# Order of two products in the middle of a Strassen pair: A12's product with B21 moved ahead of the second sum's product

## The chip, the cores and the metric

The kernel runs on one NeuronCore of a Trainium2 chip. The metric is device time in microseconds (us) for one launch; the figure for the kernel before is the median of three runs. The engines are named as the profile names them: PE (TensorE matmuls), PEld (its weight loads), DVE (VectorE), ACT (ScalarE), POOL (GpSimd) and SP (SyncE, whose queue issues nearly all DMAs).

## The reference, cut to what matters

```python
scale = cond @ norm_w.T + 1.0
ms = mean(x * x, axis=-1)
h = x * (scale[:, None, :] * rsqrt(ms + EPS))     # x: (4, 1024, 512)
val, gate = split(h @ up_w.T, 2, axis=-1)         # up_w: (4096, 512)
h = val * gelu(gate)                              # (4, 1024, 2048)
hq = act_quant(h)                                 # per token: round(h * 127 / max|h|), scaled back
wq = weight_quant(down_w)                         # -1, 0 or 1 times one scale
y = hq @ wq.T                                     # down_w: (512, 2048)
return y + x
```

## The kernel before, in words

The four batch items are handled one after the other. For each, the 2048 hidden features are cut in 16 blocks of 128; one block of one item is a slot (`slot`, line 648), and all 1024 tokens of the item go through it as two halves of 512. Item 0 runs with plain matmuls (`plain_half`); items 1 to 3 run the up-projection as a Strassen-Winograd scheme of 7 products per slot instead of 8. Each such product (`product`, line 574; matmuls at line 580) is six matmuls of 128x512 into a PSUM bank called A, B or E.

The down-projection of an item is done while a later item's slots run. It is a Strassen-Winograd scheme too (class `Pair`, line 812). One pair takes 128 tokens of each half (A11, A12 are the first half's quantized features 0 to 1023 and 1024 to 2047; A21, A22 the second half's) and the ternary weight blocks B11, B12, B21, B22, with sums of activations S1 to S4 (`sum1` at line 827, `sums` at lines 834 to 836, all on DVE) and sums of weights T1 to T4. Each of its seven products (`Pair.product`, line 839; matmuls at line 848) is eight matmuls of 128x256, one half of a PSUM bank. A pair has three banks k1, k2, k3 of one pool of three ("po" in the profile), and goes in four steps:

- `first`: S1·T1 into k3's first half, A11·B11 into k3's second half; ACT copies the latter into both halves of k1 (line 858).
- `third`: S2·T2 is added to k1's second half; ACT copies that half into k2's second half (line 865); A12·B21 is added to k1's first half; DVE adds k3's first half to the two residual tiles xr (line 889, twice).
- `fourth`: S4·B22 into k1's second half, S3·T3 into k2's second half; ACT copies that into k2's first half (line 875); DVE adds k1 to xr (line 889).
- `fifth`: A22·T4 into k2's first half; DVE adds k2 to xr (line 889); SP stores both tiles (line 884).

Each engine works through its own queue in the order of the program text; a wait holds whatever stands behind it on that engine. A writer of a PSUM tile waits for earlier readers of that tile, also where the halves differ.

There are eleven pairs. Items 0 and 1 have four each, in slots 10 to 13 of items 1 and 2. In such a slot PE runs: `first`, up-products 0, 4 and 1, product 3 of the slot before, product 5, `third`, product 2 of the slot before (into E), `fourth`, product 6, `fifth`. ACT runs, around `third`, the copy of A at line 658 (after product 5), the copy of line 865, and then work of the next item's tokens that a planner (`Filler`, line 1204) hands out: squares (line 514), scaling (line 526), and high parts (line 559). POOL multiplies what line 526 leaves (line 527) and forms sums (lines 535 to 538). DVE has, besides the pair's steps, the maxima of the quantization (lines 714, 716) and the low parts of the next tokens (line 563) between its own steps of the slot (lines 678, 688, 694, 697). `next_pair` (line 1353) puts S1 of the next pair on DVE right after `fourth`.

Item 2 has three pairs, "old", after the last slot (lines 1432 to 1502). Between `third` and `fourth` of old pair 0 stands `first` of old pair 1; of old pair 1, `fifth` of pair 0, product 2 and `first` of pair 2; of old pair 2, `fifth` of pair 1 and eight plain matmuls of line 800. The fourth tile of item 2 and all of item 3 use plain matmuls (line 800). The kernel ends with item 3's quantization (lines 772 to 784) beside these matmuls ("po_end").

Of the kernel before, what the change touches and what calls it, by code (L numbers as in the profile page):

```python
# [50 lines left out]
def glu_quant_kernel(  # L51
# [760 lines left out]
    class Pair:  # L812
# [47 lines left out]
        def third(self, xrs, dq):  # L860

            k1, k2, k3 = self.banks
            self.xrs, self.dq = xrs, dq
            self.product(self.s[2], "T2", k1, 1, False, True)
            ACT.copy(k2[:, HALF:], k1[:, HALF:])  # L865
            self.product(self.part(0, 1), "B21", k1, 0, False, True)
            for h in range(2):
                self.onto(h, k3[:, :HALF], slice(HALF, D))

# [697 lines left out]
```

## Time and profile before

| what | value |
|---|---|
| median of 3 runs | 736.64 us (736.18 to 737.06) |
| the profiled execution's own time | 738.6 us |
| its span, first to last instruction | 736.8 us |
| mean granted TensorE clock | 0.997 |
| DVE busy | 580.1 us (79%), 819 instructions |
| ACT busy | 399.5 us (54%), 629 instructions |
| POOL busy | 195.8 us (27%), 207 instructions |
| line 848, matmuls of 128x256 | 269 to 283 ns each, median 272 or 273 |
| line 865, ACT copies of 128x256 | 11, 357 to 358 ns each, from 286.2 to 693.9 us |
| line 858, ACT copies of 128x512 in the first four pairs | 572 ns each |

How to read it: the span is the stretch that the trace covers; the medians come from runs without a profile, and a saving on the chain that ends last comes off either. A matmul's duration is longer than the distance at which the next one starts, because matmuls are pipelined; what a row of eight costs is read from the start of one row to the start of the next. A line of the timeline gives start, duration, engine, source line, operation, output and inputs, the count of merged instructions, and in brackets the idle time of that engine before it and what ended it.

### The profile page before, as it was taken

What the parts mean: (1) busy time and instruction counts of PE and PEld (TensorE: products, weight loads), DVE (VectorE), ACT (ScalarE), POOL (GpSimd) and SP (SyncE); (2) the same over time, 40 slices, a digit from 0 to 9 for tenths busy, and PEclk for the clock granted to TensorE, in tenths of its full rate; (3) what the DMA queues carried; (4) which work ended last, traced back from release to release, by engine and by line L of the source; (5) the groups of instructions that cost most, each with busy time, mean ns of one, the idle gap of its engine ahead of it and who ended that gap; (6) DMA issues with size and microseconds to landing.
All of it is one profiled execution on the core that took longest, in us unless ns stands there. A gap on an engine that the chain in (4) does not pass through costs nothing.

```text
span 736.8 us, 10143 instructions
## 1 busy us (share of the span) xinstructions
PE 721.8 (98%) x3662; PEld 360.4 (49%) x3662; DVE 580.1 (79%) x819; ACT 399.5 (54%) x629; POOL 195.8 (27%) x207
## 2 busy tenths in 40 slices
PE   6999999999999999999999999999999999999998
PEld 3544444444444446555444445665444444445744
DVE  5877888885698899787689897677678888756797
ACT  4868875872336674544335677443433666332264
POOL 1379887775100034340010031460020000000100
PEclk9999999999999999999999999999999999999999
DMA  6749999988344564766735647765934555442253
GB/s 225 257 130 324 279 276 264 246 204 228 115 101 101 129 147 132 196 169 152 184 100 102 130 102 180 190 148 147 231 94 105 88 118 101 101 100 86 99 175 114
DMA packets 203982, 117.30 MB, mean 159 GB/s; under 512 B 165382, under 2 KB 174487, under 8 KB 203932
## 3 DMA queue, kind: packets, MB, share of 16 engines
q1 hardware_dynamic: 203642, 116.33, 62.8%
q8 instruction: 28, 0.46, 0.3%
q10 hardware_dynamic: 290, 0.33, 0.1%
q14 instruction: 22, 0.18, 0.1%
HBM read 54.22 MB, written 23.09 MB: 105 GB/s over the span
## 4 chain that ended last, share of the span: by engine, by line
PE 89%; DVE 7%; DMA 1%; ACT 1%; issue 1%; SPq 0%; ACTq 0%; DVEq 0%
PE A L580 31%; PE E L580 16%; PE pg L595 10%; PE pv L595 10%; PE B L580 8%; PE po L848 8%; PE po_end L800 4%; DVE gm L714 1%; DVE R L716 1%; PE po L800 1%; DMA H<-in_x_dram 1%; PE ptx L939 1%; DVE R L709 1%; DMA SXY<-H 1%; DVE H L678 0%
## 5 line engine op out<-in xcount | busy, mean ns | idle before, releaser
L580 PEld LDWEIGHTS <-SXY 128*128 128x128 f16 x2016 | 197.2, 98 | 232.3 <-issue 0.7
L580 PE MATMUL A<-R,SXY 128*128 128x512 f16 x1152 | 266.3, 379 | 0.0
L580 PE MATMUL E<-R,SXY 128*128 128x512 f16 x576 | 140.0, 379 | 0.1
L678 DVE SCALAR_TENSOR_TENSOR H<-A,sg,t 128x512 f32<-128x512 f32 x48 | 36.0, 750 | 72.7 <-PE A L580 72.5
L730 POOL PARTITION_ALL_REDUCE am<-R x8 | 14.4, 1794 | 234.7 <-DVE R L716 234.7
L772 DVE TENSOR_TENSOR H<-H,am 128x1024 f32<-128x1024 f32 x64 | 76.2, 1217 | 0.0
L595 PEld LDWEIGHTS <-SXY 128*128 128x128 f16 x486 | 47.5, 98 | 57.5 <-DMA SXY<-H 0.8
L580 PE MATMUL B<-R,SXY 128*128 128x512 f16 x288 | 70.0, 379 | 0.0
L714 DVE TENSOR_REDUCE gm<-H 128x512 f32<-128x1024 f32 x56 | 69.0, 1233 | 1.0
L691 ACT ACTIVATE t<-t,sg 128x512 f32<-128x512 f32 x48 | 34.7, 724 | 63.9 <-DVE t L688 63.8
L595 PE MATMUL pg<-R,SXY 128*128 128x512 f16 x252 | 57.8, 379 | 0.3 <-DMA SXY<-H 0.3
L595 PE MATMUL pv<-R,SXY 128*128 128x512 f16 x234 | 54.4, 379 | 0.0
L848 PE MATMUL po<-wd,R 128*128 128x256 fp8e4 x384 | 49.7, 272 | 4.6 <-ACT po L865 4.6
L675 ACT ACTIVATE t<-B,sg 128x512 f32<-128x512 f32 x48 | 33.1, 689 | 36.4 <-PE B L580 36.4
L484 POOL TENSOR_SCALAR ssq<-ssq 128x2 f32<-128x2 f32 x12 | 4.2, 351 | 177.7 <-ACT xt L514 124.9
L658 ACT COPY t<-A 128x512 f32<-128x512 f32 x48 | 28.0, 584 | 39.4 <-PE A L580 39.1
L780 ACT ACTIVATE H<-H 128x1024 f32<-128x1024 f32 x38 | 40.0, 1052 | 15.6 <-DVE H L772 15.5
L848 PEld LDWEIGHTS <-R 128*128 128x128 bf16 (+1 forms) x416 | 40.6, 98 | 15.3 <-issue 7.0
L670 ACT COPY v<-E 128x512 f32<-128x512 f32 x48 | 28.2, 587 | 31.1 <-PE E L580 27.6
L716 DVE TENSOR_TENSOR R<-R,gm 128x512 f32<-128x512 f32 x56 | 42.7, 762 | 1.3
L697 DVE SCALAR_TENSOR_TENSOR H<-v,sg,t 128x512 f32<-128x512 f32 x48 | 37.5, 781 | 8.0 <-ACT t L691 8.0
L666 ACT COPY B<-A 128x512 f32<-128x512 f32 x48 | 27.5, 574 | 25.4 <-PE A L580 25.0
(208 smaller groups left out, 988.2 us busy)
## 6 DMA issues: line engine op xcount, KB each, us to landing
SXY<-s_dram SPq DMA_DIRECT2D x57, 256.0 KB, 3.1
s_dram<-SXY SPq DMA_DIRECT2D x18, 384.0 KB, 3.2
H<-in_L_cond_up_w_dram SPq DMA_DIRECT2D x13, 512.0 KB, 5.4
SXY<-s_dram SPq DMA_DIRECT2D x39, 128.0 KB, 3.1
xr<-in_x_dram SPq DMA_DIRECT2D x19, 256.0 KB, 3.0
out_dram<-xr SPq DMA_DIRECT2D x19, 256.0 KB, 2.4
H<-in_x_dram SPq DMA_DIRECT2D x8, 512.0 KB, 8.0
R<-in_L_cond_down_w_dram SPq DMA_DIRECT2D x8, 512.0 KB, 6.3
```

Source lines behind the costliest of these rows:

```text
L580: PE.matmul(o, s[:, w, k, :], tv[:, :, c, l, k, :], start=start and n == 0, stop=stop and n == len(TERMS) - 1, skip_group_check=True,)
L595: PE.matmul(ps, a[k // 2][:, w, k % 2, :], XP[:, l, k, h * TOK : (h + 1) * TOK], start=n == 0, stop=n == len(terms) - 1,)
L675: ACT.activation(cur["t1"], pb, AF.Gelu, scale=gain(g, 1))
L678: DVE.scalar_tensor_tensor(h_half(g - 1, 0), prev["A"], gain(g - 1, 0), prev["t1"], ALU.mult, ALU.mult)
L691: ACT.activation(prev["t2"], prev["t2"], AF.Gelu, scale=gain(g - 1, 1))
L697: DVE.scalar_tensor_tensor(h_half(g - 1, 1), prev["v"], gain(g - 1, 0), prev["t2"], ALU.mult, ALU.mult)
L714: DVE.tensor_reduce(gm[0], v, AX.X, ALU.max, apply_absolute_value=True)
L716: return [largest, lambda: DVE.tensor_tensor(m, m, gm[0], ALU.max)]
L772: DVE.tensor_tensor(v, v, r.to_broadcast([P, 2, TOK]), ALU.mult)
L780: ACT.activation(v, v, AF.Copy, bias=MAGIC)
L800: PE.matmul(po.rearrange("p (y c o) -> p y c o", c=2, o=P), q[:, a, h, j], wd8[:, :, j // n, j % n, :, y0:y1].rearrange("p c o y -> p y c o"),
L848: PE.matmul(po, w[:, j], m, start=start and j == 0, stop=stop and j == n - 1, skip_group_check=True,)
```

## The change

Inside `Pair.third` one line moves up. The product A12·B21 into k1's first half is issued first, then S2·T2 into k1's second half, and then the copy of that half into k2. The number and kind of instructions on every engine stay the same, and so does the order on DVE, POOL, SP and ACT. On PE two groups of eight matmuls, with their weight loads, change places in each of the eleven pairs. The copy's line number becomes 866.

```diff
             k1, k2, k3 = self.banks
             self.xrs, self.dq = xrs, dq
+            self.product(self.part(0, 1), "B21", k1, 0, False, True)
             self.product(self.s[2], "T2", k1, 1, False, True)
             ACT.copy(k2[:, HALF:], k1[:, HALF:])
-            self.product(self.part(0, 1), "B21", k1, 0, False, True)
             for h in range(2):
                 self.onto(h, k3[:, :HALF], slice(HALF, D))
```

In the list of instructions of the changed program, the semaphore wait for ACT that stood on the first matmul of A12·B21 stands on the first matmul of S4·B22 (in `fourth`) for the pairs inside slots.

## The prediction

> **What bounds the kernel.** I read the engines' shares, then the chain of work that ended last, then PE's waits, then the timeline around them.
>
> ```profile
> PE 721.8 (98%) x3662; PEld 360.4 (49%) x3662; DVE 580.1 (79%) x819; ACT 399.5 (54%) x629; POOL 195.8 (27%) x207
> ...
> PE 89%; DVE 7%; DMA 1%; ACT 1%; issue 1%; SPq 0%; ACTq 0%; DVEq 0%
> ```
>
> PE is busy for 98% of the span and carries 89% of the chain. So PE's few idle stretches are what can be won. The list of PE's waits (total us, times, longest):
>
> ```profile
> PE po L848 <- ACT po L865: 4.6, 10, 0.5
> PE ptx L939 <- DVE H L934: 2.8, 1, 2.8
> ...
> PE po_B L848 <- ACT po_A L865: 0.5, 1, 0.5
> ...
> PE po L848 <- DVE H L827: 0.3, 1, 0.3
> ```
>
> The largest one is the pair's own: eleven times, once per pair, PE waits for the copy of line 865. The timeline of the first pair's middle (slot 10 of item 1) shows who waits:
>
> ```profile
> 285.15 1.04 PE L848 MATMUL po<-wd,R 128*128 128x256 fp8e4 x8
> ...
> 286.23 0.36 ACT L865 COPY po<-po 128x256 f32<-128x256 f32 x1 [0.29 <-PE po L848]
> 286.50 1.34 ACT L526 ACTIVATE H<-H,rs 128x512 f32<-128x512 f32 x2
> 286.63 1.03 PE L848 MATMUL po<-wd,R 128*128 128x256 fp8e4 x8 [0.44 <-ACT po L865]
> ...
> 287.50 1.46 PE L580 MATMUL E<-R,SXY 128*128 128x512 f16 x6
> ...
> 288.80 1.04 PE L848 MATMUL po<-wd,H 128*128 128x256 fp8e4 x8
> ...
> 289.67 1.04 PE L848 MATMUL po<-wd,R 128*128 128x256 fp8e4 x8
> ...
> 290.80 0.36 ACT L875 COPY po<-po 128x256 f32<-128x256 f32 x1 [2.96 <-PE po L848]
> ```
>
> S2·T2 starts at 285.15; the copy waits for its end; A12·B21 writes the other half of the same bank and waits for the copy. Product 2 (E) and S4·B22 (288.80) follow without a gap.
>
> **What is removed.** Eight matmuls of line 848 cost 0.87 us from start to start (288.80 to 289.67). From S2·T2 to A12·B21 it is 286.63 - 285.15 = 1.48 us, so each middle loses 0.61 us. (The view's 0.44 leaves out 0.17 by which the last matmul normally overlaps its successor: 1.04 - 0.87.) The other seven pairs inside slots show 1.48 or 1.49; the three old pairs 1.53 or 1.54 (678.83 to 680.36, for one), a loss of 0.66. Together 8 x 0.61 + 3 x 0.66 = 6.86 us. With A12·B21 first no reader of k1 stands between the two products, and the stall goes.
>
> **What is added.** The next writer of k1 is S4·B22, which now waits for the copy. Counted from the start of `third`: before, the copy ended at 286.23 + 0.36 - 285.15 = 1.44. After, S2·T2 starts at 0.87, the copy ends at 2.31, product 2 starts at 1.74, takes 1.30 (287.50 to 288.80), and S4·B22 is due at 3.04. The cover is product 2 alone, with 0.73 us to spare; without it each pair would wait 0.57. In the old pairs at least sixteen matmuls (1.74 us) stand between, and the spare time is about 1.1. Cost: 0.
>
> **What moves on ACT.** The copy comes 0.87 us later after the start of `third`, and holds back what is queued behind it: line 526 or 559, then the copy of line 875, then the gelu of line 691. `fourth` comes 0.61 earlier, so ACT's idle time before line 875 shrinks by 1.48. It is 2.96, 1.19, 2.97 and 4.22 in item 1's four pairs and the same within 0.01 in item 2's. Only the pair in slot 11 falls short, by 0.29; A22·T4, which waits for that copy, starts 0.68 after it ended (307.62 against 306.58 + 0.36), so 0.39 is left. Cost: 0.
>
> **What moves elsewhere.** No DMA changes its place on SP. The DVE queue has the same order; line 889 after `third` reads k3, finished long before. S2 is wanted 0.87 later than before. POOL's line 527 follows ACT's line 526: 0.87 later in slot 10, 0.87 - 0.61 = 0.26 later in slot 11, 0.35 earlier in slot 12.
>
> **What is late next.** PE becomes earlier by 0.61 per pair; the question is whether DVE follows. In slots 11 and 12 of item 1 it hardly can:
>
> ```profile
> 305.69 0.48 DVE L889 SCALAR_TENSOR_TENSOR xr<-po,dq,xr 128x256 f32<-128x256 f32 x1 [0.41 <-DMA xr<-in_x_dram]
> ...
> 319.71 1.76 DVE L716 TENSOR_TENSOR R<-R,gm 128x512 f32<-128x512 f32 x1
> ...
> 323.44 1.21 DVE L827 TENSOR_TENSOR H<-R 128x1024 bf16<-128x1024 bf16 x1
> ...
> 324.70 1.05 PE L848 MATMUL po<-wd,H 128*128 128x256 fp8e4 x8 [0.26 <-DVE H L827]
> ...
> 488.18 0.75 DVE L678 SCALAR_TENSOR_TENSOR H<-A,sg,t 128x512 f32<-128x512 f32 x1 [1.91 <-PE A L580]
> ```
>
> From 305.69 to 324.65 DVE works with hardly a gap (0.13 us at 308.62), and S1 of the fourth pair (line 827) comes last: PE already waits for it before S1·T1 at 324.70. PE's own work would bring it there 3 x 0.61 + 0.42 = 2.25 earlier (0.42: 323.41 to 324.70 less 0.87). DVE's run begins with the landing of xr at 305.69. SP issues that load in an unbroken row of DMAs that begins at 292.04, when product 6 of slot 10 has ended, so it comes only slot 10's 0.61 earlier; with the gap of 0.13 closed DVE gains at most 0.74. But its operations there are stretched beside POOL (line 716 takes 1.76 where 0.69 is its usual time, line 827 takes 1.21 against 0.68), and POOL and DVE now shift by different amounts: one more meeting with a POOL sum (0.73 us each) would leave nothing. So S1·T1 of that pair comes between 0 and 0.74 earlier, with the far end at 0.7 later if two such meetings are added. I take 0.4, the middle of the two nearer ends, because both engines shift by parts of one slot only. With slot 13's own 0.61, item 1 gives 1.0 (bounds -0.1 and 1.35).
>
> The Trainium skill ("SBUF — State Buffer", "Who interferes with whom") says that a DVE instruction with two SBUF inputs and a GpSimd instruction that reads SBUF lock each other out for a whole instruction. The 1.76 of line 716 agrees: it ends 0.55 after POOL's operation does. Played through by that rule, POOL being 0.26 later in slot 11, lines 827 and 697 meet it anew and S1·T1 moves by about 0.3 (an estimate), which makes the sum 5.3 in place of 5.4.
>
> In item 2 DVE waits for PE in slot 12 (1.91 us before line 678, last row above), so it goes with PE again. The tight place is S1·T1 in slot 12, due at 481.92 - 1.22 = 480.70; line 827 ended at 480.49 and moves with xr, 0.61, unless POOL holds it, up to one operation of line 527 (1.25). I take nothing lost, 8 x 0.61 / 2 = 2.4; bound 1.9.
>
> The old pairs give 3 x 0.66 = 2.0. There DVE's steps follow PE: its idle time before line 889 is ended by PE at 688.27 (0.59), 698.93 (0.45) and 704.14 (0.33). After that DVE and ACT quantize with little idle time and PE's po_end matmuls never wait; should the quantization gain only what the first two pairs give it (1.24 at 688.27), 1.5 would be left, as PE needs its results within a few tenths of their making.
>
> Sum: 1.0 + 2.4 + 2.0 = 5.4 us. The profiled execution has 738.6 (span 736.8); its span would become 731.4. The median lies 0.2 under the span; 736.64 - 5.4 = **731.2 us**.
>
> **Rivals.** (1) Nothing becomes late: all 6.86 us come back, 729.8. For it: PE's waits on DVE sum to 0.3 in all slots. Against: the unbroken DVE run to 324.65.
> (2) More is late: DVE behind POOL's lock takes item 1's gain (0.6 left), one pair of item 2 loses its 0.61 and the end keeps 1.5: 0.6 + 1.8 + 1.5 = 3.9, 732.7. For it: the stretched rows. Against: DVE's idle time in item 2 and before each line 678 in slot 13 (3.13).
> (3) Slower: S4·B22 waits for the copy, since only product 2 covers it. It starts to wait once the copy is 0.73 late, and eats the gain from 1.34 on. At 2.0 late each pair in a slot loses 0.66: 8 x 0.66 less the old pairs' 2.0 is +3.3, 739.9. Against it: ACT was idle for 0.29 before this copy in all eight and waited for PE, and will stand idle longer now.
> (4) The change does nothing: PE's wait would have to move to S2·T2. Its first matmul has no new wait for ACT in the changed program; S4·B22 has it.
>
> **How the numbers follow.** Forecast 0.55; rival 1 0.22; rival 2 0.16; no change 0.04 (rival 4, or rival 3 in part); slower 0.03. Two kernels within 0.2% (1.5 us; the three runs differ by 0.9) can't be told apart. The first three lie beyond that: faster 0.93, same 0.04, slower 0.03. The range runs from rival 1 less half the runs' scatter, 729.4, to the low bounds together (-0.1 + 1.9 + 1.5 = 3.3, 733.3) with some scatter, 733.6.
>
> **What would show it.** Right: no wait of line 848 for the copy in PE's list; 1.74 us from A12·B21's start to product 2; S4·B22 without idle time; PE's wait for line 827 before slot 13 of item 1 grown from 0.26 to about 1.5 to 2.1. Wrong: a wait of S4·B22 for line 866; of A22·T4 for line 875; new idle time in item 2's slot 12 or among po_end matmuls.

## The result, and the profile after

| | median us | lowest to highest |
|---|---|---|
| before, 6 runs | 736.41 | 735.96 to 738.72 |
| changed, 6 runs | 732.36 | 730.86 to 733.86 |

The ratio is 0.9941, 95% interval 0.9922 to 0.9960: the changed kernel is faster by 4.1 us, which lies inside the predicted range. The profiled execution took 731.92 us (span 730.1), 6.7 less than the one before. A second measurement, told below, gave 0.9924 (0.9907 to 0.9942).

The page's shares and the chain after:

```profile
PE 719.6 (99%) x3662; PEld 359.0 (49%) x3662; DVE 580.9 (80%) x819; ACT 398.5 (55%) x629; POOL 195.9 (27%) x207
...
PE 85%; DVE 6%; POOL 3%; DMA 3%; ACT 1%; issue 1%; SPq 1%; POOLq 0%; DVEq 0%; ACTq 0%
```

PE still sets the end. PE's waits (total us, times, longest) after:

```profile
PE ptx L939 <- DVE H L934: 2.2, 1, 2.2
PE po L848 <- DVE H L827: 1.5, 2, 0.8
```

No wait for the copy is left, of eleven. What has grown is the wait for line 827, S1 of the next pair: from 0.3 in one place to 1.5 in two. The first pair's middle on the timeline after (start, duration, engine, line, idle time before in brackets):

```profile
283.86 1.91 PE L848 MATMUL po<-wd,R 128*128 128x256 fp8e4 x16
...
285.61 1.46 PE L580 MATMUL E<-R,SXY 128*128 128x512 f16 x6
...
285.81 0.36 ACT L866 COPY po<-po 128x256 f32<-128x256 f32 x1 [1.16 <-PE po L848]
...
286.90 1.04 PE L848 MATMUL po<-wd,H 128*128 128x256 fp8e4 x8
...
288.90 0.36 ACT L875 COPY po<-po 128x256 f32<-128x256 f32 x1 [1.50 <-PE po L848]
```

Both products now run as one row of sixteen matmuls, 1.75 us from start to start of what follows (before: 2.35). The copy ends at 286.17, and S4·B22 starts at 286.90 as its place in the row asks, 0.73 later. ACT's idle time before line 875 fell from 2.96 to 1.50.

**Where the time went, stage by stage.** PE's rows give the start of each stage in the two profiled executions:

| stage | before, us | after, us | gain |
|---|---|---|---|
| start of the span to slot 10 of item 1 | 278.68 | 277.38 | 1.30 |
| slots 10 to 13 of item 1 (278.68 to 340.49; 277.38 to 337.30) | 61.81 | 59.92 | 1.89 |
| from there to slot 10 of item 2 | 110.74 | 110.73 | 0.01 |
| slots 10 to 13 of item 2 (451.23 to 512.62; 448.03 to 507.94) | 61.39 | 59.91 | 1.48 |
| from there to the first old pair's `third` | 166.21 | 166.21 | 0.00 |
| `third` of the first old pair to the first po_end matmul | 26.77 | 24.80 | 1.97 |
| po_end to the end of the span | 31.2 | 31.2 | 0.0 |

The pairs gave 5.34 us. The 1.30 in front of them lies in code that the change doesn't touch; it is a difference between executions (see the last section). So the single profiled pair of executions overstates the gain, and a stretch that begins after the start compares kernels more sharply than the whole span. The experiments are compared by such a stretch too: from the first S1·T1 in slot 10 of item 1 to the first po_end matmul. It took 428.67 us before (276.93 to 705.60) and 423.31 after (275.64 to 698.95).

**The new wait.** In slot 11 of item 1 after the change:

```profile
302.79 0.48 DVE L889 SCALAR_TENSOR_TENSOR xr<-po,dq,xr 128x256 f32<-128x256 f32 x1 [0.96 <-DMA xr<-in_x_dram]
...
303.82 2.51 POOL L527 TENSOR_TENSOR xn<-xn,sc 128x512 f32<-128x512 f32 x2 [4.14 <-ACT xn L526]
...
304.17 0.49 DVE L889 SCALAR_TENSOR_TENSOR xr<-po,dq,xr 128x256 f32<-128x256 f32 x1 [0.89 <-DMA xr<-in_x_dram]
...
305.12 1.04 PE L848 MATMUL po<-wd,R 128*128 128x256 fp8e4 x8
...
305.82 1.05 DVE L827 TENSOR_TENSOR H<-R 128x1024 bf16<-128x1024 bf16 x1
...
306.93 1.05 PE L848 MATMUL po<-wd,H 128*128 128x256 fp8e4 x8 [0.78 <-DVE H L827]
```

A22·T4 starts at 305.12, S1·T1 should follow 0.87 later, at 305.99, and starts at 306.93: 0.94 lost. Line 827 was late twice over. DVE had idled 1.85 us for the two xr tiles, and then line 827 took 1.05 instead of 0.68, ending 0.54 after POOL's line 527 (303.82 + 2.51 = 306.33). Item 2 has the same picture with 0.94 lost:

```profile
474.47 2.50 POOL L527 TENSOR_TENSOR xn<-xn,sc 128x512 f32<-128x512 f32 x2 [4.14 <-ACT xn L526]
...
476.03 1.48 DVE L827 TENSOR_TENSOR H<-R 128x1024 bf16<-128x1024 bf16 x1
...
477.57 1.05 PE L848 MATMUL po<-wd,H 128*128 128x256 fp8e4 x8 [0.77 <-DVE H L827]
```

### The profile page after: what moved, and what is told of

It reads as the page before. It is cut to its first block, busy times and chain, and to the rows that moved or that the text cites. A ratio compares the mean times of both kernels' runs of the same rounds, so it can differ in the third digit from the quotient of the medians.

```text
span 730.1 us, 10143 instructions
## 1 busy us (share of the span) xinstructions
PE 719.6 (99%) x3662; PEld 359.0 (49%) x3662; DVE 580.9 (80%) x819; ACT 398.5 (55%) x629; POOL 195.9 (27%) x207
## 4 chain that ended last, share of the span: by engine, by line
PE 85%; DVE 6%; POOL 3%; DMA 3%; ACT 1%; issue 1%; SPq 1%; POOLq 0%; DVEq 0%; ACTq 0%
PE A L580 33%; PE E L580 17%; PE po L848 8%; PE B L580 8%; PE pg L595 6%; PE pv L595 6%; PE po_end L800 4%; DVE gm L714 1%; DMA s_dram<-R 1%; PE po L800 1%; DMA H<-in_x_dram 1%; POOL H L372 1%; DMA SXY<-H 1%; DVE R L716 1%; ACT H L313 1%
## 5 line engine op out<-in xcount | busy, mean ns | idle before, releaser
L670 ACT COPY v<-E 128x512 f32<-128x512 f32 x48 | 28.1, 586 | 31.2 <-PE E L580 27.7
L716 DVE TENSOR_TENSOR R<-R,gm 128x512 f32<-128x512 f32 x56 | 40.9, 730 | 1.3
L784 ACT ACTIVATE R<-H 128x1024 bf16<-128x1024 f32 x38 | 40.1, 1055 | 0.8
```

Of the source, the lines that this page charges most:

```text
L716: return [largest, lambda: DVE.tensor_tensor(m, m, gm[0], ALU.max)]
L784: ACT.activation(q, by_tile(v), AF.Copy, bias=-MAGIC)
```

## The experiments

Theory A: the gain is the eleven stalls and nothing else, less what S1's lateness takes. The rivals: part of the gain is paid back outside the pairs; the end of the kernel hides the old pairs' share; DVE is the limit, so that the loss before S1·T1 can't be removed; the copy's cover is not what the count says. For the new wait, two causes had to be told apart, the late landing of xr and POOL.

| kernel | ratio to before, 95% interval | stretch, us | less than before |
|---|---|---|---|
| changed, again | 0.9924 (0.9907 to 0.9942) | 422.36 | 6.31 |
| new order in slots only | 0.9951 (0.9934 to 0.9967) | 425.29 | 3.38 |
| new order in old pairs only | 0.9976 (0.9964 to 0.9989) | 427.03 | 1.64 |
| changed, S1 earlier | 0.9898 (0.9880 to 0.9915) | 421.41 | 7.26 |
| changed, xr loaded earlier | 0.9915 (0.9891 to 0.9940) | 422.55 | 6.12 |
| changed, without line 527 | one run, 728.72 us | 421.69 | 6.98 |
| changed, without the cover | one run, 735.40 us | 426.50 | 2.17 |
| before, S1 earlier | one run, 738.36 us | 428.23 | 0.44 |

One sum closes the account. In each execution add up what PE lost: wherever a row of line 848 is followed late, the distance to the start of the next row less the 0.87 us that eight matmuls normally take. That gives 7.28 us before, 1.88 after, and 0.94, 3.86, 5.62, 0, 1.14, 0.46, 5.12 and 6.86 in experiments 1 to 8. The stretch less this loss is 421.37 to 421.43 us in nine of the ten executions (421.23 in experiment 6). So the stretch differs between the kernels by the waits for the copy and for S1, and by nothing else of more than 0.2 us.

**1. The changed kernel again.** No edit.

> The changed kernel once more, to size the gain. Theory A (the gain is the eleven stalls, less two waits of 0.94 us for S1 before S1·T1 in slot 12): 61.81 - 59.92 = 1.9 in item 1, 61.39 - 59.91 = 1.5 in item 2, 2.0 in the old pairs, 5.3 us in all, ratio 0.9928. Rival B (part of it is paid back somewhere outside the pairs, as the medians 736.41 and 732.36 say): 4.1 us, ratio 0.9945.

The ratio supports A: 731.66 against 737.10 us, 5.4 us; the rival's 0.9945 lies just outside the interval, and the stage table shows nothing paid back outside the pairs. In this execution item 2 had no wait for S1 at all and item 1 the same 0.94, hence 6.31 in the stretch instead of 5.36. So whether S1 is late varies between executions. In item 2 line 827 was issued at 474.81, ahead of POOL's second multiplication, and took 0.68; POOL's two took 3.00 instead of 2.51:

```profile
473.62 3.00 POOL L527 TENSOR_TENSOR xn<-xn,sc 128x512 f32<-128x512 f32 x2 [4.15 <-ACT xn L526]
...
474.81 0.68 DVE L827 TENSOR_TENSOR H<-R 128x1024 bf16<-128x1024 bf16 x1
```

Whoever came first kept the other waiting. POOL's second multiplication began at 474.86, only 0.05 us after line 827.

**2 and 3. The change in parts.**

```diff
-            self.product(self.part(0, 1), "B21", k1, 0, False, True)
+            first = self.b < B - 2        # experiment 3: self.b == B - 2
+            if first:
+                self.product(self.part(0, 1), "B21", k1, 0, False, True)
             self.product(self.s[2], "T2", k1, 1, False, True)
             ACT.copy(k2[:, HALF:], k1[:, HALF:])
+            if not first:
+                self.product(self.part(0, 1), "B21", k1, 0, False, True)
```

> New order in the eight pairs inside slots, old order in the three old pairs. Theory A: 3.4 us, ratio 0.9954; three stalls of 0.66 us of line 848 for the copy remain. If the late pairs hide their stall behind the last quantization, this kernel equals the changed one.

> New order in the three old pairs only. Theory A: 2.0 us, ratio 0.9973. Rival: the end of the kernel is set by VectorE and ScalarE, so less than 1 us, ratio above 0.9986.

Both ratios are A's within their intervals, and 0.9951 and 0.9976 together make the whole change's 0.9924 within theirs. The ratios alone would leave room for the rivals (0.9941, the changed kernel's first ratio, and 0.9986 lie inside the intervals); the stretches don't. With the slots alone it is 1.98 longer than with the whole change (425.29 against 423.31), three times 0.66. In that execution three waits for the copy remained (1.0 + 0.5 us idle) and two for line 827. With the old pairs alone the stretch fell by 1.64, not 1.98: in this execution three pairs in slots of the old order waited for S1 too (0.22 to 0.27 each, where the kernel before had one of 0.42). The old pairs' share reaches the end of the kernel: the quantization moves up with them.

**4. S1 ahead of line 889.** The lowest median of the study.

```diff
-                mid = [lambda: (pair.third(xrs, dq), d_sums(late_sums)), lambda: (pair.fourth(), next_pair()), lambda: (loads(), pair.fifth())]
+                mid = [lambda: (next_pair(), pair.third(xrs, dq), d_sums(late_sums)), lambda: pair.fourth(), lambda: (loads(), pair.fifth())]
```

> The changed kernel with S1 of the next pair put on VectorE ahead of the two steps of line 889 that follow third, instead of after fourth. Theory A: the waits before S1·T1 in slot 12 go, 2 x 0.94 = 1.9 us below the changed kernel, 7.2 below the kernel before, ratio 0.990. Rival: VectorE is the limit of slots 11 and 12, so the same time reappears as a wait of another product (S2·T2 or S4·B22) and the ratio equals that of the changed kernel.

0.9898: 729.76 us, 1.9 below the changed kernel on the same chip (731.66), though the two intervals overlap. Its stretch is 1.90 and 0.95 shorter than those of the changed kernel's two profiled executions, which had two waits and one. PE's list has no wait of line 848 at all. Slot 11 of item 1 in this kernel's timeline:

```profile
301.63 0.69 DVE L827 TENSOR_TENSOR H<-R 128x1024 bf16<-128x1024 bf16 x1
...
303.84 0.48 DVE L889 SCALAR_TENSOR_TENSOR xr<-po,dq,xr 128x256 f32<-128x256 f32 x1 [0.49 <-DMA xr<-in_x_dram]
...
305.71 1.04 PE L848 MATMUL po<-wd,H 128*128 128x256 fp8e4 x8
```

Line 827 ends at 302.32, 3.4 us before S1·T1; DVE still waits for xr, but nothing that PE needs soon stands behind that wait. The stretch is shorter by 7.26: the eleven stalls (6.86) and the 0.42 that the kernel before lost at slot 13 make 7.28. That DVE is the limit there is refuted.

**5. xr loaded earlier.** The turn of the next item's first tokens moves behind slot 11's loads in SP's queue.

```diff
-                (None, p0, ((6, "z"), (7, "x"), (7, "y"), (9, "y"), (10, "x"), (10, "z"))),
+                (None, p0, ((6, "z"), (7, "x"), (7, "y"), (9, "y"), (10, "x"), (11, "x"))),
```

> The changed kernel with the transposing DMA of the next item's first tokens (line 566, some 4.7 us on SP's queue) issued after slot 11's two loads of xr instead of before them. If the late landing of xr is what makes S1 late in slot 12: VectorE no longer idles for xr before line 889 in slot 11 (0.96 + 0.89 and 1.22 + 0.20 us), the two waits of 0.94 before S1·T1 go, 1.9 us gained. If POOL's lock alone makes it late (line 827 takes 1.05 and 1.48 in place of 0.68): the waits stay above half their size.

The waits for xr in slot 11 and both waits of 0.94 went, as a late xr predicts. (In item 1 line 827 now waited 0.95 for the transposing DMA that had moved; it started at 304.66, ahead of POOL's second multiplication, and took 0.73. So this experiment removes the meeting with that multiplication together with the late xr.) But 1.9 us did not come: slot 13 of item 1 lost 1.14 (322.05 - 320.04 - 0.87). This kernel's timeline there:

```profile
316.98 2.97 POOL L527 TENSOR_TENSOR H<-H,sc 128x512 f32<-128x512 f32 x2 [2.02 <-ACT H L526]
317.04 1.77 DVE L716 TENSOR_TENSOR R<-R,gm 128x512 f32<-128x512 f32 x1
...
320.71 0.73 POOL L536 TENSOR_TENSOR H<-H 128x256 f32<-128x256 f32 x1
320.78 1.21 DVE L827 TENSOR_TENSOR H<-R 128x1024 bf16<-128x1024 bf16 x1
...
322.05 1.05 PE L848 MATMUL po<-wd,H 128*128 128x256 fp8e4 x8 [0.97 <-DVE H L827]
```

Lines 716 and 827 each came 0.06 or 0.07 us after a POOL operation had begun, and were stretched to 1.77 and 1.21 (0.69 and 0.68 without POOL). Together that is 1.61 us, more than the 1.14 lost. The ratio, 0.9915, can't be told from the changed kernel's or from experiment 4's.

**6. Without POOL's multiplication.**

```diff
                     ACT.activation(xn[:, h], xn[:, h], AF.Copy, scale=r)
-                    POOL.tensor_tensor(xn[:, h], xn[:, h], sc, ALU.mult)
```

> The changed kernel without POOL's multiplication of line 527 for items 2 and 3 (their tokens then lack the condition's scale). If the late xr makes S1 late: PE still waits before S1·T1 in slot 12, by about 0.5 in item 1 (line 827 would end 0.37 earlier) and 0.2 in item 2. If POOL is the whole cause, both waits go.

This kernel leaves out the condition's scale, so its result is not the reference's; and its line numbers behind line 527 are lower by one. One wait of 0.3 us was left, in item 1 (0.46 lost: 304.88 - 303.55 - 0.87), and none in item 2. In item 1 that is in number what was expected of a late xr alone (0.5), in item 2 less (0.2). But in item 1 line 827 (826 here) was stretched again, by one of POOL's sums, which now come earlier:

```profile
303.55 0.73 POOL L535 TENSOR_TENSOR xt<-xn 128x256 f32<-128x256 f32 x1
...
303.89 0.93 DVE L826 TENSOR_TENSOR H<-R 128x1024 bf16<-128x1024 bf16 x1
...
304.88 1.05 PE L847 MATMUL po<-wd,H 128*128 128x256 fp8e4 x8 [0.30 <-DVE H L826]
```

With 0.68 instead of 0.93 about 0.2 would have been lost (an estimate). So this experiment doesn't measure xr's lateness by itself.

What the two causes do is better read from the five places where 0.94 was lost (both items after the change, item 1 in experiment 1, both items in experiment 2). Line 827 was issued there between 0.17 and 0.81 us before S1·T1 was due and took 1.05 to 1.69; it always ended 0.55 after POOL's second multiplication of line 527, and 0.87 to 0.89 after the due time. So POOL sets the size of the loss. The late xr matters because line 827 then stands behind the start of that multiplication, 0.93 or 0.94 before the due time. Where line 827 came ahead of that start (item 2 in experiment 1, item 1 in experiment 5), nothing was lost in that slot. A late xr costs less without POOL: in slot 11 of item 1 in experiment 7, DVE idled 2.13 us for xr, line 827 met no POOL operation (0.68), and 0.24 was lost.

**7. Without the cover.**

```diff
-                mid = [lambda: (pair.third(xrs, dq), d_sums(late_sums)), lambda: (pair.fourth(), next_pair()), lambda: (loads(), pair.fifth())]
+                mid = [lambda: (pair.third(xrs, dq), d_sums(late_sums), pair.fourth()), lambda: next_pair(), lambda: (loads(), pair.fifth())]
```

> The changed kernel with fourth moved ahead of product 2 in the eight slots, so that S4·B22 follows S2·T2 at once. By the prediction's count the copy ends at 2.31 us after the start of third and S4·B22 is due at 1.74: PE waits 0.57 + 0.04 per pair, eight times, and the gain of those slots (0.61 each) is gone. If the wait doesn't hang on the copy: no wait for line 866.

PE's timeline in the first pair of this kernel:

```profile
284.14 1.91 PE L848 MATMUL po<-wd,R 128*128 128x256 fp8e4 x16
286.50 1.03 PE L848 MATMUL po<-wd,H 128*128 128x256 fp8e4 x8 [0.44 <-ACT po L866]
```

S4·B22 was due at 284.14 + 1.74 = 285.88 and started at 286.50: 0.62 lost against 0.61 expected, and eight waits for line 866 in PE's list (3.6 us idle). The wait does hang on the copy, and product 2 is all that hides it. It is the same stall as before the change, in another place. The stretch is still 2.17 shorter than before, of which the old pairs, whose cover stays, have 1.98.

**8. The kernel before with S1 earlier.** The edit of experiment 4, on the old order.

> The kernel before with S1 put ahead of the two steps of line 889 as in the other experiment. The wait of line 848 for line 827 in slot 13 of item 1 (0.26 of idle time, 0.42 us lost) goes or stays small; the eleven waits for the copy stay. So at most 0.4 us faster than the kernel before: the late S1 costs nothing much there.

The stretch fell by 0.44; the eleven waits for the copy stayed (4.6 + 0.5 us idle) and the one for line 827 went. Its one run, 738.36 us, shows nothing of it: slot 10 began 0.22 later than in the profile of before. The early S1 is worth 0.4 us with the old order and 0.95 or 1.90 with the new one (two executions): what the change took away had been hiding most of S1's lateness.

## Why the prediction was right, and where it was not

- *The stall and its size.* Right. Experiments 2, 3 and 4 add up to eight times 0.61 and three times 0.66.
- *S4·B22 behind product 2, 0.73 to spare.* Right to the digit: 286.90 - 286.17. Experiment 7 takes the cover away and measures 0.62 for the predicted 0.61.
- *ACT.* Right in kind. Idle time before line 875 fell to 1.50, 1.49 and, in slot 11, nothing; A22·T4 started 0.50 after that copy's end (305.12 against 304.26 + 0.36), where 0.39 was counted.
- *Old pairs 2.0.* Measured 1.97; the doubt about the last quantization (1.5) was not borne out.
- *Item 1, 1.0 with bounds -0.1 and 1.35.* Mis-sized, and outside the bounds: 1.89. The prediction placed the wait before slot 13, grown to 1.5 to 2.1. It was not there at all. It came a slot earlier, 0.94 before S1·T1 of slot 12, and a PE delayed there was no longer ahead of S1 in slot 13. So 2.44 + 0.42 - 0.94 = 1.92 was left. The step that failed is DVE's shift, "at most 0.74". Counted from the start of slot 10, line 827 of slot 12 ended 1.79 earlier than before (324.65 - 278.68 against 321.56 - 277.38). The xr tile, taken as 0.61 earlier, gave only 0.22 of that (305.69 and 304.17); line 716 of slot 12 gave 1.08, because it no longer met POOL (0.68 us instead of 1.76). The prediction allowed for meetings that are added, and not for one that goes:

```profile
317.97 0.68 DVE L716 TENSOR_TENSOR R<-R,gm 128x512 f32<-128x512 f32 x1
...
320.61 0.95 DVE L827 TENSOR_TENSOR H<-R 128x1024 bf16<-128x1024 bf16 x1
```

- *Item 2, 2.4 with bound 1.9.* Mis-sized, and outside the bound: 1.48. The prediction named the very place, S1·T1 of slot 12, and took nothing lost; POOL held line 827 for 1.48 us. A second execution lost nothing there. Behind the bound stands a misread row. In the profile of before, S1·T1 of slot 12 starts at 481.05; 481.92, from which the prediction counts, is the row after it, A11·B11:

```profile
481.05 1.04 PE L848 MATMUL po<-wd,H 128*128 128x256 fp8e4 x8
481.92 1.04 PE L848 MATMUL po<-wd,R 128*128 128x256 fp8e4 x8
```

So it was due at 481.05 - 1.22 = 479.83 and not at 480.70, and line 827, at 480.49 - 0.61 = 479.88, was just late even without POOL. The same count for item 1, which the prediction doesn't make, gives 308.50 - 1.22 = 307.28 against 308.03 - 0.61 = 307.42. The prediction's own working, with the right row, points at slot 12 in both items. New idle time in item 2's slot 12 was one of its signs of being wrong, and it came.

- *Sum.* 5.4 predicted, 5.34 in the pairs' stages of the profiled execution. Two errors of 0.9 in opposite directions cancelled, which is luck; the sum is better than its parts deserve. Both come from S1 in slots 11 and 12. DVE's time there was carried forward as a block that shifts, while its stretched rows belong to meetings with POOL that a shift of some tenths makes or breaks. The medians gave 4.1 and 5.4 us.
- *A small misreading.* Of the three idle times given for the old pairs, the one at 698.93 was ended by ACT's line 780, not by PE. Nothing hung on it.

The Trainium skill ("SBUF — State Buffer", "Who interferes with whom") says that a DVE instruction with two SBUF inputs and a GpSimd instruction that reads SBUF exclude each other for a whole instruction, and that issue order decides who waits. The rows agree: line 827 at 476.03, issued while POOL's line 527 ran, took 1.48; issued just before it in the repeat, it took 0.68 and POOL waited. Played through in the prediction, the rule gave one right meeting (line 827 in slot 11 of item 1) and one that did not come (line 697 there took 0.73, before 1.12), and 0.3 for S1·T1 of slot 13, which moved 1.28 earlier from the start of slot 10. In item 2 the landing of one DMA chose the side.

The rivals: (1), all 6.86 back, is what the change gives once S1 is out of the way (experiment 4). (2) had the right mechanism, S1 behind xr and POOL, in the wrong slots. The first measurement's median, 732.36, lies nearer its 732.7 than the forecast's 731.2, but its parts, 0.6, 1.8 and 1.5, were 1.89, 1.48 and 1.97. (3), S4·B22 waiting for the copy, needs the cover gone (experiment 7), and even then the kernel is not slower than before (one run, 735.40 us against a median of 737.02).

## What to carry to other kernels

When a matmul waits for an engine that still reads the same PSUM bank, put work for that bank that needs no wait ahead of the read, and check what stands between the read and the bank's next writer: that is the new cover, and its spare time can be counted from the rows. Then ask which engine was hidden by the stall; here VectorE's next sum came next, and moving it ahead of a step that waits for a DMA gave another 0.95 to 1.90 us of the stretch. Do not carry stretched instructions forward as fixed durations: when two engines shift by different amounts, decide each meeting anew and keep the whole meeting as uncertainty.

## What the runs showed of the hardware that was not expected

The stretch from 9 to 15 us, the kernel's first transposes, ran at different TensorE clocks in executions whose code is the same there (columns of this view: the window; its length; busy time and count of PE, PEld, DVE, ACT, POOL; granted clock; DMA share; GB/s). Before the change:

```profile
9.00:15.00 6.00, 3.42 (x18) 3.43 (x19) 4.03 (x17) 3.12 (x8) 2.30 (x3) 0.75 0.81 301
```

After:

```profile
9.00:15.00 6.00, 3.14 (x23) 2.28 (x22) 4.37 (x18) 4.11 (x10) 2.31 (x3) 1.00 0.76 284
```

With a granted clock of 0.74 to 0.80 there the sixteen transposes took 2.46 to 3.62 us (before, experiments 2, 3, 7 and 8), with 1.00 they took 1.96 or 1.97 (after, experiments 1, 4, 5 and 6). The first S1·T1 of slot 10 came at 275.92 to 277.37 us in the five executions with the low clock and at 274.06 to 275.64 in the five with the full one, with the same matmuls ahead of it. That is a part of the scatter between runs.

Five of the six profiled kernels with the new order in all pairs drew the full clock, and none of the four others. The runs on record speak for chance. Each has its mean granted clock, and in the ten profiled executions 0.998 or less goes with the low clock at the start. Of the 24 runs of the kernel before that stand beside the experiments, 20 have 0.999 or 1.000 (735.79 to 738.41 us) and four have 0.998 or less (738.64 to 739.25). Of the changed kernel's twelve, four have 0.998 (732.80 to 733.86 us); the others took 730.13 to 732.73. So the low start costs time with either order, and the change doesn't bring the full clock.
